# A fixed order of TensorE's work per head that begins three heads earlier in an attention block

## The chip, the cores and the metric

The kernel runs on one core of one Trainium2 chip. The metric is the device time of one execution in microseconds. A core has TensorE (PE, matrix products, with its weight loads shown as PEld), VectorE (DVE), ScalarE (ACT), GpSimd (POOL) and SyncE (SP). Here SP only issues DMA transfers; POOL issues some of them too and does a little elementwise work. The engines run side by side, each through its own list of instructions, and wait for each other by semaphores.

## The reference

The whole kernel is two transformer layers on `x` of 4 rows x 512 tokens x 512 channels: a gate, a state-space mixer, a gate, a mixture of experts, then a gate, attention, a gate and a feed-forward block. The change lies in the attention of the second layer:

```python
q = einsum('bsh,he->bse', x, w_q).reshape(b, sq, GROUPS, HPG, KVC)   # 4 groups x 4 heads x 128
kv = einsum('bsh,he->bse', x, w_kv)                                  # one key and one value per group
scores = einsum('bqgpd,bkgd->bgqpk', q, k) * SCALE
scores = where(causal, scores, -inf)
probs = softmax(scores, axis=-1)
ctx = einsum('bgqpk,bkgd->bqgpd', probs, v).reshape(b, sq, HEADS * KVC)
out = einsum('bse,eh->bsh', ctx, w_dense)                            # added to x
```

Here `x` stands for the gated input `h`. All numbers are 32-bit floats.

## The kernel before, in words

Attention runs over 64 heads in one Python loop, which is unrolled into the program: group `g` (0 to 3) outside, row of the batch `b` (0 to 3) within it, head of the group `i` (0 to 3) within that. This document counts them 0 to 63 in that order, so heads 12 to 15 are the last row of group 0, and head 16 is the first of group 1. A head is worked in these steps, which are spread over several turns of the loop:

- Queries. In group 0, `queries` makes the query of one head from `h` with four 128x512 products (L1726). From group 1 on, `two_queries` makes those of two heads with seven products of half size instead of eight (L1749), as a fast matrix product of 2x2 blocks; for it VectorE adds up the parts (L1752), and it needs sums of blocks of `h`, kept as `ht`, and of the weights, which POOL forms in `pair_weights` (L1518 to L1521) after the weights of the pair have been loaded (L1504). A call of `lead` records one half of a pair: four products, or three.
- Keys and values. `keys_` and `values` (L1699, L1710), once per group and row.
- Scores. `scores` makes four blocks of 128 queries (L1798, 128 to 512 columns, as the causal mask needs no more). VectorE adds the mask (L1801), takes the maximum (L1803), ScalarE the exponential (L128), VectorE scales (L1809, L1810) and transposes 32x32 blocks into `turned` (L1814). POOL then issues four transfers of `turned` to device memory (L1822).
- Between the blocks of scores, `nudge` adds a piece of the gates of later stages to VectorE and ScalarE (L259 to L333).
- Collecting. A later turn loads the transposed probabilities back as `pT` (L1840). This load is written to come after the last instruction recorded on POOL, and there are two `pT` buffers.
- Context. Three turns after the scores, `context` multiplies `pT` with the values (L1867), and ScalarE copies the result to `cx` (L1878). When the fourth head of a row is there, `dense` multiplies the four contexts with `w_dense` in four parts (L1886), each of which VectorE adds to `x` (L1894).

The order of the instructions on each engine is chosen when the program is built, by priority and by modelled readiness of operands, except where the code binds it. `after(nc.tensor)` binds an instruction behind the last one recorded on TensorE. `in_turn()` does so when the flag `even[0]` is set, and is wrapped around the paired queries, scores, contexts and dense parts. With the flag set, TensorE's order is the order in which the loop records the work, and three things differ from before: `ahead` records the queries of later heads in halves and the next row's keys and values, each in a fixed place after the scores of a head; one dense part is recorded per turn; and nothing is left to the builder. Without it, a row's dense product is recorded in one go, and queries go wherever the builder puts them. In this kernel the flag is set for groups 1 to 3, up to the last two heads.

The buffers that matter: `cx` has five buffers of its own, and four buffers `rr` that first hold results of the experts, loaded by `look_ahead` and added to `x` by `combine` during group 0; from group 1 on, contexts of rows 0 and 2 use the latter. `load_row` reloads `h` and `ht` of a row for the next group on SP's queue, at places given by a small table in the loop.

Of the kernel before, what the change touches and what calls it, by code (L numbers as in the profile page):

```python
# [19 lines left out]
B, T, C = 4, 512, 512  # L20
NC = C // P
# [24 lines left out]
HEADS, GROUPS, KVC = 16, 4, 128  # L46
# [37 lines left out]
def block_kernel(ctx: ExitStack, tc: tile.TileContext, a: dict, out: bass.AP):  # L84
    nc = tc.nc

    @contextmanager
    def after(*engines):

        with ExitStack() as es:  # L90
            for e in engines:
                last = next(
                    (i for i in reversed(nc.cur_bb.bb.instructions) if i.engine == e.engine), None
                )
                if last is not None:
                    es.enter_context(tc.issue_after(last))
            yield
# [48 lines left out]
    def ps_tp(name):  # L146
        return ps.tile([P, 512], F32, tag="tp", name=name, bufs=2)
# [755 lines left out]
    with ExitStack() as ph:  # L903
        right = dict(bufs=1, side="right", reuse_waits="tile")
        wx = early.enter_context(tc.tile_pool(name="ssm_wx", **right))
        even = early.enter_context(tc.tile_pool(name="ssm_even", **right))
# [211 lines left out]
        def start_tile(w, t):  # L1118
            u = Tile_()
            u.w, u.t = w, t  # L1120
            u.tok = slice(t * P, (t + 1) * P)
            u.first, u.last = t == 0, t == NT - 1

            u.zs = []
            for hh in range(2):
                pz = ps_mm("pz")
                for k in range(NC):
                    nc.tensor.matmul(  # L1128
                        pz,
                        lhsT=w.h[:, k, u.tok],  # L1130
                        rhs=wzt[:, k, hh * 512 : (hh + 1) * 512],
                        start=(k == 0),
                        stop=(k == NC - 1),
                    )
                zs = sm.tile([P, 512], F32, tag="zs", name="zs", bufs=3)
                act(zs, pz, AF.Silu)
                u.zs.append(zs)
            return u
# [209 lines left out]
        u = start_tile(w, 0)  # L1348
# [6 lines left out]
        for b in range(B):  # L1355
# [6 lines left out]
            for t in range(NT):  # L1362
# [97 lines left out]
                old, u = u, nxt  # L1460
# [100 lines left out]
    with tc.tile_pool(name="moe_w2", bufs=1, reuse_waits="tile") as wm:  # L1561
# [33 lines left out]
        n = len(nc.cur_bb.bb.instructions)  # L1595
# [15 lines left out]
    with att as ph:  # L1611
# [70 lines left out]
        even = [False]  # L1682

        def in_turn():
            return after(*[nc.tensor] * even[0])
# [34 lines left out]
        def new_q(i):  # L1720
            return sm.tile([P, T], F32, tag=f"q{i % 2}", name="qT", bufs=2)

        def queries(u, i):
            pq = ps_tp("pq")
            for k in range(NC):
                nc.tensor.matmul(  # L1726
                    pq,
                    lhsT=u.wq[:, i // 2, k, i % 2 * KVC : (i % 2 + 1) * KVC],
                    rhs=u.hk[:, k, :],
                    start=(k == 0),  # L1730
                    stop=(k == NC - 1),
                )
            qT = new_q(i)
            nc.scalar.mul(qT, pq, SCALE)
            return qT
# [95 lines left out]
        def new_pT():  # L1831
            return sm.tile([P, QUAD, SLOTS, SQ], F32, tag="pT", name="pT")
# [12 lines left out]
        def context(u, prs):  # L1845

            if isinstance(prs, list):
                pT = new_pT()
                for qi, pr in enumerate(prs):
                    n = (qi + 1) * P  # L1850
                    ptp = ps_tp("ptp")
                    for kj in range(qi + 1):
                        nc.tensor.transpose(
                            ptp[:, kj * P : (kj + 1) * P], pr[:, kj * P : (kj + 1) * P], ident
                        )
                    nc.any.tensor_copy(
                        pT[:, :, 3 * qi : 4 * qi + 1, :].rearrange("p r k j -> p k r j"),
                        ptp[:, :n].rearrange("p (k r j) -> p k r j", r=QUAD, j=SQ),
                    )
            else:  # L1860
                if id(prs) not in back:
                    collect()
                pT = back.pop(id(prs))
            pctx = ps_acc("pctx")
            with in_turn():
                for kj in range(NT):
                    nc.tensor.matmul(  # L1867
                        pctx[:, kj * P :].rearrange("p (q r j) -> p q r j", r=QUAD, j=SQ),
                        lhsT=u.v[:, kj, :],
                        rhs=pT[:, :, 4 * kj : 10 + kj : 3, :].rearrange("p r q j -> p q r j"),  # L1870
                        start=(kj == 0),
                        stop=(kj == NT - 1),
                    )
            if u.g == 0 or u.b % 2 or (u.g, u.b) == (GROUPS - 1, 2):
                cx = sm.tile([P, T], F32, tag="cx", name="cx", bufs=5)
            else:
                cx = cb.tile([P, T], F32, tag=f"rr{len(u.ctxT) % 2}", name="cx", bufs=2)
            nc.scalar.copy(cx, pctx)  # L1878
            u.ctxT.append(cx)
# [40 lines left out]
        heads_ = [(g, b, i) for g in range(GROUPS) for b in range(B) for i in range(HPG)]  # L1920

        def begin(n):
            g, b, i = heads_[n]
            if (g, b) not in groups:
                groups[g, b] = start_group(g, b, weights[g])
            u = groups[g, b]
            if i == 0 and not hasattr(u, "kT"):
                keys_(u)
                values(u)
            if g == 0:  # L1930
                return u, queries(u, i)
            if (g, b, i) == (1, 0, 0):
                lead(n)
                lead(n)
            return u, qs.pop((g, b, i))

        def lead(s):
            g, b, i = heads_[s]
            if (g, b) not in groups:
                groups[g, b] = start_group(g, b, weights[g])  # L1940
            if (g, b, i) not in making_q:
                making_q[g, b, i] = two_queries(groups[g, b], i // 2)
                qs[g, b, i] = next(making_q[g, b, i])
            else:
                qs[g, b, i + 1] = next(making_q.pop((g, b, i)))
# [28 lines left out]
        ready, held = begin(0), []  # L1974
        for n, (g, b, i) in enumerate(heads_):
            u, qT = ready
            if g == 0 and i == 0 and b + 1 < B:
                combine(b + 1, (0, 1))
                look_ahead(b + 1, (2, 3))
            if g == 0 and i == 3 and b + 2 < B:  # L1980
                look_ahead(b + 2, (0, 1))
            if g == 2 and i == 0 and b < 3:
                to, name = ((ffg_d, "gateT"), (ffu_d, "upT"), (ffd_d, "downT"))[b]
                nc.sync.dma_start(out=to, in_=a[name])
            s = n + ({2: 6} if g else {0: 4, 3: 5} if b == B - 1 else {}).get(i, len(heads_))
            if s < len(heads_):
                hs[heads_[s][:2]] = load_row(heads_[s][1])
            if loading:
                at, rest = loading.pop()
                pairs_w[at] = next(rest)  # L1990
            if (b, i) == (B - 1, 0) and g + 1 < GROUPS:
                weights[g + 1] = load_group(g + 1)
            pair = ((B - 1, 0), (B - 1, 3)) if g == 0 else ((B - 2, 3), (B - 1, 1))
            if (b, i) in pair and g + 1 < GROUPS:
                at = g + 1, pair.index((b, i))
                loading.append((at, pair_weights(*at)))
                next(loading[0][1])
            if n + 1 < len(heads_):
                ready = begin(n + 1)
            if g == 0 and i == 2 and b + 1 < B:  # L2000
                act.use(act.EXP)
                h = gated(2, b + 1, x[b + 1], gp, tag="h", name=f"h2_{b + 1}")
                hs[0, b + 1] = h, None
                act.use(act.LOG_EXP)
                mix(b + 1, h)
            even[0] = g > 0 and (g, b, i) < (GROUPS - 1, B - 1, 2)
            prs = scores(u, i, qT)
            if g == 0 and i == 1 and b + 1 < B:
                with after(nc.scalar):
                    combine(b + 1, (2, 3))  # L2010
            ahead(n)
            held.append((u, prs))
            if len(held) > 3:
                settle()
            dense_parts(2 if g == GROUPS - 1 and (b, i) >= (2, 2) else 1)
            if n == len(heads_) - 2:
                last_row_over = [
                    i for i in nc.cur_bb.bb.instructions if i.engine == nc.scalar.engine
                ][-1]
# [13 lines left out]
    with ExitStack() as ph:  # L2033
# [96 lines left out]
        with tc.If(n_odd > 0):  # L2130
            with ExitStack() as gen:
                wl = gen.enter_context(tc.tile_pool(name="ff_gen", bufs=2, **right))
                for b in range(B):
                    h = gated(3, b, x[b], gp, tag="h", name=f"h4_{b}")
                    hd = []
                    for i in range(NFF):
                        cs = slice(i * P, (i + 1) * P)
                        pv = []
                        for name in ("gateT", "upT"):
# [5 lines left out]
                            for k in range(NC):  # L2145
                                nc.tensor.matmul(
                                    pv[-1], lhsT=w[:, k, :], rhs=h[:, k, :],
                                    start=(k == 0), stop=(k == NC - 1),
# [7 lines left out]
                    for m in range(NC):  # L2156
# [6 lines left out]
                        for i in range(NFF):  # L2163
                            nc.tensor.matmul(
                                po, lhsT=w[:, i, :], rhs=hd[i], start=(i == 0), stop=(i == NFF - 1)
# [71 lines left out]
```

## Time and profile before

| what | value |
|---|---|
| time, median of 3 runs | 2247.05 us (2238.36, 2247.05, 2247.62) |
| the profiled execution: its time, its span | 2251.16 us, 2248.9 us |
| granted TensorE clock in the profiled execution, mean | 0.972 |
| attention's first and last score-side matmul on PE (queries of group 0; dense of group 3) | from 1135.6, to 2001.9 us |
| first paired query of group 1 | 1324.7 us |
| the costliest group of matmuls, dense L1886 | 227.9 us busy |

The profile was taken by the hardware profiler on one execution. Times are from the start of the span. A row of the timeline gives start, duration, engine, line, operation, output and inputs, shape and count, and in brackets how long the engine had been idle before it and what ended that. On TensorE each 32-bit matmul leaves two records, so four matmuls are "x8". The windows view gives for stretches of time the busy time of each engine with its number of instructions, then the granted TensorE clock, the mean busy share of the 16 DMA engines and the rate in GB/s.

### The profile page before, as it was taken

Reading aid. Unit: us, or ns where it says so; the run is one execution under the profiler, and the core shown is the slowest. Engines: PE = TensorE matmul, PEld = TensorE weight load, DVE = VectorE, ACT = ScalarE, POOL = GpSimd, SP = SyncE. Lnnn points to the kernel's source line nnn. Section 1 sums busy time; section 2 is a strip of 40 time slices with the busy share of each in tenths; the row PEclk is TensorE's granted clock in tenths of the full one; section 3 lists DMA queues with packets and bytes.
Section 4 is the critical chain, followed back from the end, with each engine's and each line's share of the span. In section 5 each row is a group of like instructions: output and inputs, shape, how many; then the busy total and the mean of one; then the engine's idle time right before and its main releaser. Section 6 shows DMA issues by size and latency. Waiting matters only on the chain.

```text
span 2248.9 us, 24719 instructions
## 1 busy us (share of the span) xinstructions
PE 2130.9 (95%) x7858; PEld 1292.5 (57%) x7858; DVE 1586.8 (71%) x3207; ACT 953.9 (42%) x1875; POOL 495.0 (22%) x668
## 2 busy tenths in 40 slices
PE   5879999999999999999988998999999999999998
PEld 2545565555665444444444555666666666568887
DVE  8698889989753557576579875788788866655332
ACT  4575666665842233333155432333333322333221
POOL 4022232322322111222133222212212221200000
PEclk9989989999999999999989998999999999999999
DMA  7542241342333457988578675777777665521100
GB/s 261 182 138 68 94 163 67 116 152 76 131 127 126 145 201 274 370 297 303 201 235 269 214 255 186 211 213 224 209 221 235 193 206 165 206 104 38 38 19 20
DMA packets 125512, 390.99 MB, mean 174 GB/s; under 512 B 15360, under 2 KB 36224, under 8 KB 111872
## 3 DMA queue, kind: packets, MB, share of 16 engines
q1 hardware_dynamic: 90560, 249.60, 32.1%
q0 software_dynamic: 32512, 135.55, 19.3%
q10 hardware_dynamic: 2304, 4.20, 0.5%
q8 instruction: 65, 1.06, 0.2%
q14 instruction: 71, 0.58, 0.1%
HBM read 363.07 MB, written 116.39 MB: 213 GB/s over the span
## 4 chain that ended last, share of the span: by engine, by line
PE 43%; DVE 4%; DMA 1%; ACT 1%; issue 1%; POOL 0%; SPq 0%; DVEq 0%; POOLq 0%
PE pd L1886 10%; PE pq L1749 6%; PE pctx L1867 6%; PE psc L1798 5%; PE pv L1710 2%; PE pk L1699 2%; PE pfo L2067 2%; PE pfo L2066 2%; PE pfg L2066 2%; PE pfg L2067 2%; PE pfu L2066 2%; PE pfu L2067 2%; PE pq L1726 1%; DMA pT<-turned 1%; DVE turned L1814 1%; DVE nmax L1803 1%
## 5 line engine op out<-in xcount | busy, mean ns | idle before, releaser
L128 ACT ACTIVATE pr<-psc,nmax 128x128 f32<-128x128 f32 (+3 forms) x256 | 134.3, 526 | 345.3 <-DVE nmax L1803 344.8
L1822 POOL DMA_DIRECT2D turned<-turned x248 | 135.7, 554 | 579.2 <-DVE turned L1814 491.3
L1886 PE MATMUL pd<-cx,wd 128*128 128x512 f32 x512 | 227.9, 593 | 0.0
L1798 PE MATMUL psc<-kT,qT 128*128 128x128 f32 (+3 forms) x512 | 158.6, 447 | 15.4 <-ACT pr L128 15.3
L1894 DVE TENSOR_TENSOR xr<-xr,pd 128x512 f32<-128x512 f32 x64 | 43.9, 686 | 176.3 <-PE pd L1886 176.2
L1057 PE MATMUL pc<-h,wxb 128*128 128x512 f32 x320 | 148.3, 619 | 5.8 <-DVE h L406 4.9
L1867 PE MATMUL pctx<-pT,v 128*128 128x512 f32 (+3 forms) x512 | 149.9, 436 | 2.9 <-DMA pT<-turned 2.9
L1886 PEld LDWEIGHTS pd<-cx,wd 128*128 128x128 f32 x512 | 93.9, 191 | 100.2 <-issue 98.6
L1867 PEld LDWEIGHTS pctx<-pT,v 128*128 128x128 f32 x512 | 96.5, 192 | 67.1 <-issue 40.8
L847 PE MATMUL po<-w,yT 128*128 128x512 f32 x296 | 134.1, 593 | 0.2 <-ACT yT L840 0.2
L814 PE MATMUL pg<-w,hT 128*128 128x512 f32 x296 | 134.0, 593 | 0.0
L825 PE MATMUL pn<-w,hT 128*128 128x512 f32 x296 | 133.3, 592 | 0.0
L1798 PEld LDWEIGHTS psc<-kT,qT 128*128 128x128 f32 x512 | 87.2, 194 | 68.8 <-issue 25.8
L1803 DVE TENSOR_REDUCE nmax<-psc 128x1 f32<-128x128 f32 (+3 forms) x256 | 119.8, 477 | 0.7
L1814 DVE STREAM_TRANSPOSE turned<-pr 128x128 f32<-128x128 f32 x248 | 119.3, 495 | 0.3
L1128 PE MATMUL pz<-wzt,h 128*128 128x512 f32 x256 | 115.9, 602 | 0.3 <-ACT st L1229 0.3
L1276 PE MATMUL po<-wot,yT 128*128 128x512 f32 x256 | 115.1, 603 | 0.0
L1057 PEld LDWEIGHTS pc<-h,wxb 128*128 128x128 f32 x320 | 61.5, 197 | 78.1 <-issue 72.3
L1810 DVE TENSOR_SCALAR pr<-pr,rsum 128x128 f32<-128x128 f32 (+3 forms) x256 | 103.9, 409 | 0.9
L1749 PE MATMUL pq<-ht,wq 128*128 128x256 f32 x384 | 100.3, 385 | 2.8 <-DVE us L1752 2.8
L1171 ACT ACTIVATE lm<-lm,cs 128x128 f32<-128x128 f32 x256 | 81.9, 390 | 22.1 <-DMA lm<-cs 19.5
L825 PEld LDWEIGHTS pn<-w,hT 128*128 128x128 f32 x296 | 54.8, 190 | 61.7 <-issue 61.7
(367 smaller groups left out, 4522.2 us busy)
## 6 DMA issues: line engine op xcount, KB each, us to landing
w<-in_w1x SPq DMA_DIRECT2D x76, 1024.0 KB
turned<-turned POOLq DMA_DIRECT2D x248, 208.0 KB, 4.0
pT<-turned POOLq DMA_DIRECT2D x62, 832.0 KB, 7.5
w<-in_w2x SPq DMA_DIRECT2D x38, 1024.0 KB
wb<-in_b1x SPq DMA_DIRECT2D x38, 512.0 KB
lm<-cs SPq DMA_DIRECT2D x32, 512.0 KB
kt<-in_fT SPq DMA_DIRECT2D x62, 256.0 KB
ek<-ek SPq DMA_DIRECT2D x62, 256.0 KB
```

The costliest lines, as they stand in the source:

```text
L128: nc.scalar.activation(*args, **kw)
L825: nc.tensor.matmul(pn, lhsT=hT[:, k, :], rhs=self.w1[s][1][:, k, :], start=(k == 0), stop=(k == NC - 1))
L1057: nc.tensor.matmul(pc, lhsT=wxb[:, k, m * P : (m + 1) * P], rhs=h[:, k, :], start=(k == 0), stop=(k == NC - 1),)
L1749: nc.tensor.matmul(out_, lhsT=w[:, c], rhs=xs[:, c], start=(c == 0), stop=(c == 1))
L1798: nc.tensor.matmul(psc[:, :n], lhsT=qT[:, qi * P : n], rhs=u.kT[:, :n], start=True, stop=True)
L1803: nc.vector.tensor_reduce(nmax, psc[:, :n], AX.X, ALU.max, negate=True)
L1814: nc.vector.transpose(blocks[:, :, 3 * qi : 4 * qi + 1, :].rearrange("p c k j -> p k c j"), pr)
L1822: nc.gpsimd.dma_start(out=d[:, :, r].rearrange("c i s -> i c s"), in_=blocks[r * SQ : (r + 1) * SQ].rearrange("i c k j -> i c (k j)"),)
L1867: nc.tensor.matmul(pctx[:, kj * P :].rearrange("p (q r j) -> p q r j", r=QUAD, j=SQ), lhsT=u.v[:, kj, :], rhs=pT[:, :, 4 * kj : 10 + kj : ...
L1886: nc.tensor.matmul(po, lhsT=dense_w[u.g, m][:, i], rhs=u.ctxT[i], start=(i == 0), stop=(i == HPG - 1),)
L2066: nc.tensor.matmul(out_, lhsT=w, rhs=xs[0], start=first_, stop=False)
L2067: nc.tensor.matmul(out_, lhsT=w, rhs=xs[1], start=False, stop=last_)
```

## The change

`even[0]` is now set at the top of a turn instead of before the scores, and from head (0, 3, 1) on, that is from the second head of group 0's last row. The simple queries of group 0 are wrapped in `in_turn()` too. Since `ahead` now records the first pair of group 1 in the turns of heads 13 and 14, the two calls of `lead` at the first head of group 1 are gone, and what that pair needs is recorded one head earlier: the reload of row 0, and the load and the sums of the first pair's weights (the second pair's from head 15 to head 14). Row 2 of group 0 now has its dense parts spread over four turns, so its contexts live longer; they go to the `rr` buffers.

```diff
         def queries(u, i):
             pq = ps_tp("pq")
-            for k in range(NC):
-                nc.tensor.matmul(
+            with in_turn():
+                for k in range(NC):
+                    nc.tensor.matmul(
...
-            if u.g == 0 or u.b % 2 or (u.g, u.b) == (GROUPS - 1, 2):
+            if u.b % 2 or (u.g, u.b) < (0, B - 2) or (u.g, u.b) == (GROUPS - 1, 2):
                 cx = sm.tile([P, T], F32, tag="cx", name="cx", bufs=5)
             else:
                 cx = cb.tile([P, T], F32, tag=f"rr{len(u.ctxT) % 2}", name="cx", bufs=2)
...
             if g == 0:
                 return u, queries(u, i)
-            if (g, b, i) == (1, 0, 0):
-                lead(n)
-                lead(n)
             return u, qs.pop((g, b, i))
...
             u, qT = ready
+            even[0] = (0, B - 1, 1) <= (g, b, i) < (GROUPS - 1, B - 1, 2)
...
-            s = n + ({2: 6} if g else {0: 4, 3: 5} if b == B - 1 else {}).get(i, len(heads_))
+            s = n + ({2: 6} if g else {B - 2: {3: 5}, B - 1: {3: 5}}.get(b, {})).get(i, len(heads_))
...
-            pair = ((B - 1, 0), (B - 1, 3)) if g == 0 else ((B - 2, 3), (B - 1, 1))
+            pair = ((B - 2, 3), (B - 1, 2)) if g == 0 else ((B - 2, 3), (B - 1, 1))
...
-            even[0] = g > 0 and (g, b, i) < (GROUPS - 1, B - 1, 2)
             prs = scores(u, i, qT)
```

More of the change, by code (lines that the diff above doesn't have):

```diff
@@ L1724, in queries @@
             pq = ps_tp("pq")
-            for k in range(NC):
-                nc.tensor.matmul(
[L1727 to L1732, printed above, removed]
+            with in_turn():
+                for k in range(NC):
+                    nc.tensor.matmul(
+                        pq,
+                        lhsT=u.wq[:, i // 2, k, i % 2 * KVC : (i % 2 + 1) * KVC],
+                        rhs=u.hk[:, k, :],
+                        start=(k == 0),
+                        stop=(k == NC - 1),
+                    )
             qT = new_q(i)
```

## The prediction

> **What bounds the kernel now.** I read the page's busy shares first, then the same numbers by stage, then, for the stage of the change, what TensorE waits for, and last the rows of TensorE, POOL and VectorE there.
>
> ```profile
> span 2248.9 us, 24719 instructions
> PE 2130.9 (95%) x7858; PEld 1292.5 (57%) x7858; DVE 1586.8 (71%) x3207; ACT 953.9 (42%) x1875; POOL 495.0 (22%) x668
> ```
>
> TensorE (PE) is the busiest engine, but 95% is a mean over stages. The windows view (busy time of each engine, granted clock, DMA share and rate) shows where it is less:
>
> ```profile
> 1312.72:1404.50 91.78, 79.41 (x277) 50.38 (x276) 68.06 (x171) 29.85 (x75) 24.71 (x43) 0.93 0.62 210
> 1440.00:1531.80 91.80, 91.80 (x357) 60.26 (x356) 71.17 (x198) 35.59 (x88) 23.41 (x42) 1.00 0.72 216
> 1345.53:1348.94 3.41, 0.69 (x4) 0.26 (x2) 3.02 (x11) 1.66 (x4) 0.00 (x0) 1.00 0.96 344
> 1348.94:1352.36 3.42, 3.32 (x8) 2.67 (x9) 2.00 (x5) 0.00 (x0) 2.18 (x4) 0.50 0.95 317
> 1389.90:1393.31 3.41, 1.87 (x5) 1.52 (x6) 1.81 (x5) 0.00 (x0) 1.86 (x4) 0.50 1.02 428
> 1393.31:1396.73 3.42, 3.42 (x10) 2.70 (x9) 0.42 (x1) 0.38 (x1) 0.33 (x1) 0.50 1.01 405
> ```
>
> The first row is the stretch that the change rewrites: from the end of head 12's scores to the first key product of group 1's second row (heads counted 0 to 63 over group, row, head). PE idles in it and runs at a granted clock of 0.93. The second row, as long, lies in group 1, where the fixed order already holds: PE never stops. So a microsecond saved in the first stretch should reach the end. What PE waits for between 1312 and 1410 us:
>
> ```profile
> PE pq L1749 <- DVE qT L1752: 7.3, 1, 7.3
> PE pq L1749 <- DVE us L1752: 2.8, 1, 2.8
> PE psc L1798 <- ACT pr L128: 1.2, 2, 0.8
> PE pk L1699 <- ACT pr L128: 1.0, 1, 1.0
> ```
>
> Both large waits stand at group 1's paired query products: VectorE's sums for them are queued behind softmax and gate work, while the 32 matmuls of row 2's dense product, 1355.51 to 1369.25, pass in one block in which VectorE has little to do. To two digits the five waits are 7.35, 2.83, 0.81, 0.44 and 0.95: 12.38 us. The timeline rows of PE and of POOL that I use:
>
> ```profile
> 1310.56 2.32 PE L1798 MATMUL psc<-kT,qT 128*128 128x128 f32 x8
> 1349.04 2.07 PE L1749 MATMUL pq<-ht,wq 128*128 128x256 f32 x4 [2.83 <-DVE us L1752]
> 1355.51 13.90 PE L1886 MATMUL pd<-cx,wd 128*128 128x512 f32 x32
> 1391.44 2.08 PE L1749 MATMUL pq<-h,wq 128*128 128x256 f32 x4 [7.35 <-DVE qT L1752]
> 1312.95 2.18 POOL L1822 DMA_DIRECT2D turned<-turned  x4 [17.68 <-DVE turned L1814]
> 1317.91 0.56 POOL L1840 DMA_DIRECT2D pT<-turned  x1 [2.78 <-PE pctx L1867]
> 1340.69 0.55 POOL L1822 DMA_DIRECT2D turned<-turned  x1 [10.68 <-DVE turned L1814]
> 1341.25 0.74 POOL L1521 TENSOR_TENSOR wq<-wq 128x256 f32<-128x256 f32 x1
> 1341.91 0.57 POOL L1840 DMA_DIRECT2D pT<-turned  x1
> ```
>
> POOL issues in order, and a `pT` load there (the transposed probabilities that a context needs) can stand behind a `turned` store that waits for VectorE's transposes of a later head.
>
> **What the stage loses.** Work in it, from row distances (a group's start to the next group's): two queries of group 0 at 3.44, six heads of scores at 2.16, seven contexts at 2.16, three pairs of queries at 6.03, keys 3.44, values 3.57, dense 13.74: 6.88+12.96+15.12+18.09+3.44+3.57+13.74 = 73.8 us. It took 91.78, so 18.0 are lost: 12.38 idle, and half of the 3.32+1.87+3.42 us that PE worked in the three windows at clock 0.50, 4.3; the other 1.3 go with the five restarts. That is the most this stage can give back.
>
> **The order.** The new order on PE has the same matmuls up to the same key product: contexts 8 and 9, query 14, scores 13, first half of pair 16, context 10, query 15, scores 14, second half of pair 16, keys, context 11, a dense part, scores 15, half of pair 18, values, context 12, a part, and so on. Pair 16 gets two heads of lead, and the dense block becomes four parts of 3.44. So the waits of 7.35 and 2.83, and the 2.2 on exponentials, go: VectorE's 68.06 us lie beside 73.8 of matmuls instead of being bunched. PE gets 11.2, 17.2, 14.8, 10.3 and 11.2 us per head for heads 13 to 17, VectorE needs some 11 for each (scores 1399.75 to last transpose 1411.09: 11.3).
>
> **What is late next.** The first pair's weight sums (L1518 to L1521) stand one head earlier on POOL, now behind head 11's `turned` stores and ahead of head 12's first; and the `pT` load of head 10, which went out at 1317.91, now stands behind that first store and L1521. The store waits for VectorE. There the last reciprocal of head 12 starts at 1321.26, the scaling follows (0.19+0.40), then the four transposes (1.68, from the row at 1323.74, which the new order has ahead of head 13's mask): 1323.55. POOL starts 0.29 later (as 1325.42 to 1325.71), and its step from store to load is 1.22 (1340.69 to 1341.91): load out at 1325.06. The load in that same position, at 1341.91, landed after 5.7 us, the one at 1380.76 after 5.4; so at 1330.8. PE comes to context 10 at 1312.72+2.16+2.16+3.44+2.16+3.45 = 1326.1. A new wait of 4.7 us, with query 15, scores 14 and all later heads queued behind it. Bounds: the shortest `pT` landing in the trace is 4.5, the slowest near here 10.5 (at 1382.96, beside two 1 MB loads): 3.5 to 9.5. I take 5.7, the row in the same position; row 1's loads, which met the stores at 1325.71, now go out only after query 15.
>
> By the Trainium skill, "DMA: Bandwidth & Descriptors", section "Anatomy of one DMA — SWDGE (gpsimd) path", a transfer takes 2.0 us plus bytes over 436 GB/s, so an estimate of 3.95 us for 832 KB and a wait of 2.9. The trace disagrees: none landed under 4.5.
>
> **The clock after it.** A 3.41 us window with PE busy for 0.69 was followed by one at 0.50, and one at 0.50 with 1.87 busy by another. On that grid (1325.05, 1328.46, 1331.87) the new wait leaves 1.0 busy in the first window and 1.1 in the second, so PE works at half clock from 1330.8 to 1335.3 and loses 2.2; with another phase 1.2 to 2.9. With 0.3 for the restart the new loss is 7.2 (5 to 12.5).
>
> In the Trainium skill, "TensorE: Matmul & The Clock Gate", section "Why this matters for your kernels", gaps over about 3 us bring the half clock, for one window: 1.7 us here. The trace agrees that a gap costs clock, but 2.83 us was already enough.
>
> **The other edits.** Row 2's context copies go to the buffers of the expert results (last read by the transposes at 1271.01): the same ACT copy, 0. Row 0's reload and the first pair's load are written one head earlier, but SP's queue keeps them in place: 0. The second pair's 0.5 MB load still follows query 15, which now ends near 1336.4; landing in 9.3 (its 1325.17 load) at 1346, then POOL's sums after head 14's stores end near 1350.8; pair 18 needs them at 1353.3: hidden by 2.5 us. If that cover goes, PE waits by the excess. SP holds `ht` of row 1 behind it, needed at 1376. The contexts after 10 are covered: head 13's load, again behind a store and L1521, is out near 1361 and wanted at 1370.
>
> **Sum.** 18.0 − 7.2 = 10.8 us. The profiled execution took 2251.16 (span 2248.9), 4.1 over the median 2247.05: 2240.4 as profiled, 2236.2 against the median; I say 2236.
>
> **Rivals.**
> - No new wait: the transposes of head 12 or its transfers come 5 us sooner. Then all 18.0 return: 2229. Against it: VectorE has no idle row from 1308 to 1346, so head 12 can't be sooner. 8%.
> - A slow transfer: `pT` takes 8 to 10.5. Loss 9.5 to 12.5, gain 5.5 to 8.5: 2238.5 to 2241.5. For it, 10.5 stands in the trace; against, it had 1 MB loads beside it. 12%.
> - VectorE becomes the bound: 68 us of it in 81 us is 84% against 78% in group 1, and with several waits in line a queue head holds the rest. The idle of PE moves rather than goes: gain 0 to 7, around 2243. Also where the order does nothing. 5%.
> - Slower: the hold on POOL repeats. If VectorE takes longer per head than PE does, the store of head n+2 holds each context as it holds context 10: at contexts 10 to 13 four times 7.2, 28.8 against the 18.0: 2258. It decides once VectorE needs more than 11.2 us a head several heads long. Group 1's 100% under this order speaks against it. 5%.
>
> **How the numbers follow.** The forecast has 70%, its own range 2233 to 2239. The bound of 0.5%, about what a measurement here can tell from no change, is 11.2 us, at 2235.8, so it cuts the forecast: 42 points beyond, as a landing 0.4 us sooner or a shorter stretch at half clock is enough for that, and 28 short. With the first rival 50% faster; with the slow transfer and the moved idle 45% the same; 5% slower. The range 2230 to 2243 holds the forecast, the slow transfer, part of the moved idle, and a run's scatter (2238.36 to 2247.62).
>
> **What would show it.** Right: no wait at L1749 on L1752 in this stretch; pd in groups of 8 rows; one PE gap of 4 to 6 us before `pctx`, ended by the DMA of `pT`, 13.4 us after head 12's scores; half clock for one or two windows there; the stretch at 81 us. Wrong: the gap missing or above 9 us, gaps before later contexts, a gap at pair 18 on L1520, or time moved outside the stretch.

## The result, and the profile after

The changed kernel took a median of 2231.03 us in 12 runs (2226.19 to 2236.79). The kernel before took 2242.70 in its 12 runs beside it (2237.88 to 2254.39); the three runs known ahead, with a median of 2247.05, are among those. The medians are 11.7 us apart. The ratio, which is that of the means, is 0.9943, 95% interval [0.9926, 0.996]: 12.8 us less, between 9.0 and 16.6. A second series, with 27 runs of the kernel before, gave 0.9951 [0.9933, 0.9969], 11.0 us less. So the change saves time beyond doubt; on which side of 0.5% the saving lies, neither series tells.

The profiled execution took 2229.05 us. Its page:

```profile
span 2227.1 us, 24718 instructions
PE 2115.8 (95%) x7858; PEld 1283.1 (58%) x7858; DVE 1584.9 (71%) x3207; ACT 952.4 (43%) x1875; POOL 500.2 (22%) x668
```

The same number of matmuls, and 15.1 us less of PE's busy time, of which only 3.1 are in the stretch that the change rewrites; a second execution of the kernel before, at 2120.8 busy, shows that much of the rest is scatter. The windows view of that stretch, from the end of head 12's scores to the first key product of group 1's second row (called the stage from here on), of PE's idle time in it, and of the context behind that:

```profile
1300.24:1382.08 81.84, 76.35 (x277) 48.75 (x276) 66.25 (x168) 29.65 (x75) 26.58 (x43) 0.96 0.68 221
1314.35:1317.76 3.41, 0.00 (x0) 0.00 (x0) 3.41 (x11) 1.83 (x5) 2.21 (x4) 0.87 0.78 192
1319.52:1323.81 4.29, 4.29 (x9) 2.45 (x10) 3.67 (x8) 0.78 (x2) 0.32 (x1) 0.52 0.77 316
```

The stage takes 81.84 us; it took 91.78. PE's busy time in it fell from 79.41 to 76.35 and its granted clock rose from 0.93 to 0.96. What is left of idle time is almost all in one piece, from 1314.35 to 1319.52. The second row shows its first 3.41 us, in which VectorE does not stop; the context behind it then runs at a clock of 0.52. PE's waits in the stage are two in all:

```profile
PE pctx L1868 <- DMA pT<-turned: 5.2, 1, 5.2
PE psc L1799 <- ACT pr L128: 0.3, 1, 0.3
```

Both waits at the paired queries (7.35 and 2.83) are gone. (Every line from L1727 on has moved down by one.) A new wait of 5.17 us stands before a context. The timeline of PE, then of POOL, then of VectorE:

```profile
1313.32 1.03 PE L1750 MATMUL pq<-ht,wq 128*128 128x256 f32 x4
1319.52 4.45 PE L1868 MATMUL pctx<-pT,v 128*128 128x512 f32 x8 [5.17 <-DMA pT<-turned]
1323.81 3.60 PE L1727 MATMUL pq<-h,wq 128*128 128x512 f32 x8
1337.58 3.60 PE L1887 MATMUL pd<-cx,wd 128*128 128x512 f32 x8
```

```profile
1302.66 1.56 POOL L1518 TENSOR_TENSOR wq<-wq 128x256 f32<-128x256 f32 x1
1304.20 1.69 POOL L1519 TENSOR_TENSOR wq<-wq 128x256 f32<-128x256 f32 x1
1305.86 0.76 POOL L1520 TENSOR_TENSOR wq<-wq 128x256 f32<-128x256 f32 x1
1312.53 0.55 POOL L1823 DMA_DIRECT2D turned<-turned  x1 [5.91 <-DVE psc L1802]
1313.09 0.74 POOL L1521 TENSOR_TENSOR wq<-wq 128x256 f32<-128x256 f32 x1
1313.76 0.57 POOL L1841 DMA_DIRECT2D pT<-turned  x1
```

```profile
1302.02 1.69 DVE L259 TENSOR_TENSOR_SCAN num<-decay,ekv 128x512 f32<-128x512 f32 x1
1303.63 1.68 DVE L322 SCALAR_TENSOR_TENSOR den<-den,rec 128x1024 f32<-128x1024 f32 x1
1310.54 1.68 DVE L1815 STREAM_TRANSPOSE turned<-pr 128x128 f32<-128x128 f32 x4
```

POOL's rows are the hold: it stands idle for 5.91 us at head 12's first `turned` store, and head 10's `pT` load is in line behind the store and L1521. (The view names L1802 as what ended the idle time, the VectorE row right behind the four transposes; those end at 1312.22, as VectorE's rows show.) The load goes out at 1313.76, and PE begins at 1319.52. That the load itself was ready some 11 us earlier is shown by the first experiment below. VectorE's rows show why the store waited longer than it might have: beside POOL's L1518 and L1519 the scan L259 and L322 took 1.69 and 1.68 us, and the two sums twice their usual 0.73.

Single executions scatter more than the effect, so the experiments below are also compared by two lengths from their profiled executions: the stage (here from the end of the last score row, so 91.62 before and 81.68 after), and the rest, from the stage's end to the end of the span. The scatter comes largely from ahead of the stage: attention's first key product began between 1115.1 and 1127.0 us, and from there to the stage's start it took 184.6 to 190.9, in kernels with and without the change. The stage repeats to 0.3 us: 91.62 and 91.89 for the kernel before, 81.68 and 81.54 for the changed one. The rest was 844.4 and 841.9 before, 845.0 and 844.9 after, so it repeats to some 3.

Where a stage below is compared with "the kernel before" or "the changed kernel", it is with the mean of these two profiles, 91.76 and 81.61, unless a figure is given.

| kernel | ratio to before, 95% | stage us | stage and rest us |
|---|---|---|---|
| before, again | 1.0006 [0.9986, 1.0026] | 91.89 | 933.8 |
| changed, again | 0.9951 [0.9933, 0.9969] | 81.54 | 926.4 |
| `pT` collected first | 0.9964 [0.9946, 0.9982] | 83.35 | 928.1 |
| queries in another PSUM buffer | 0.9945 [0.9927, 0.9963] | 81.36 | 924.9 |
| both | 0.9935 [0.9916, 0.9953] | 77.84 | 919.0 |
| both, row 2's dense product in one block | 0.9925 [0.9904, 0.9946] | 77.10 | 920.6 |
| both, nothing bound before group 1 | 0.9957 [0.9939, 0.9975] | 81.30 | 922.5 |
| changed, dense product in one block | 1.0005 [0.9988, 1.0022] | 83.19 | 936.2 |
| changed, nothing bound before group 1 | 1.0004 [0.9984, 1.0024] | 82.70 | 931.3 |
| changed, simple queries not bound | 0.996 [0.9943, 0.9977] | 81.69 | 926.9 |
| before, dense parts spread | 1.0007 [0.999, 1.0024] | 88.13 | 932.3 |
| before, `pT` collected first | 0.9987 [0.9966, 1.0008] | 90.95 | 932.1 |

### The profile page after: what moved, and what is told of

Read it like the earlier page. It is cut to its first block, busy times and chain, and to the rows that moved or that the text cites. A ratio compares the mean times of both kernels' runs of the same rounds, so it can differ in the third digit from the quotient of the medians.

```text
span 2227.1 us, 24718 instructions
## 1 busy us (share of the span) xinstructions
PE 2115.8 (95%) x7858; PEld 1283.1 (58%) x7858; DVE 1584.9 (71%) x3207; ACT 952.4 (43%) x1875; POOL 500.2 (22%) x668
```

## The experiments

The theory: the gain is the two waits at the paired queries, and what is left is `pT` in line on POOL. The rivals are named with each run. First the same two kernels again.

> The kernel before once more, for a second profile of the stage between head 12's scores and the first key product of group 1's second row (91.78 us in the first). If the saving lies in that stage alone, it is 91 to 93 us here too, with the waits of about 2.8 and 7.4 us at L1749 again, whatever the span; if earlier stages or the profile's luck made the difference, it will lie elsewhere or change by several us.

> The changed kernel once more. My theory (the saving is this stage: waits at the first paired queries gone, one new wait before context 10): stage 81 to 83 us, one gap of 4.5 to 6 us before pctx, ratio 0.994 to 0.997. The rival that something outside the stage changed too: the part of the span ahead of head 12's scores, or behind the first key product of row 1, differs from before by more than 2 us in the same direction in both pairs of profiles, and the ratio is under 0.994.

Measured: five waits of 0.44, 0.81, 0.94, 2.83 and 7.36 before, two of 0.32 and 4.89 after. The waits belong to the kernels, not to an execution. The rival's signs came out mixed. The part ahead of the stage was shorter in the changed kernel in both pairs of profiles, by 12.5 us (1312.88 to 1300.40) and 4.2 (1308.55 to 1304.34); the ratio, at 0.9951, was not under 0.994. What the first is worth is taken up under what stays open.

**Is the place of `pT` on POOL the cause of the new wait?** One line puts the load ahead of the pair's sums:

```diff
             if loading:
                 at, rest = loading.pop()
+                collect(1)
                 pairs_w[at] = next(rest)
```

> The changed kernel with one call added: head 10's (and later each) pT load is recorded ahead of the weight sums, so on POOL it no longer stands behind the store of head 12. Theory of the place on POOL: the gap of 5.2 us before context 10 disappears; but query 15 needs one of two tp PSUM buffers, which VectorE's sums of pair 16 free at 1322.5 in the changed kernel's profile, 8 us after PE would be there, less what VectorE gains; so I expect a wait of 3 to 5 us at L1727 on a VectorE sum instead, and a gain of only 1 to 3 us over the changed kernel. Rival, the wait is the whole cost: 5.2 and some 2 of half clock, 7 us gained. Rival, the transfer itself is the cost and not its place: the gap stays at 5 us, no gain.

The load went out right behind head 11's stores, and the sums after it:

```profile
1319.12 0.56 POOL L1841 DMA_DIRECT2D pT<-turned  x1 [0.20 <-issue]
1319.69 0.74 POOL L1518 TENSOR_TENSOR wq<-wq 128x256 f32<-128x256 f32 x1
```

PE's waits in the stage were then:

```profile
PE pq L1727 <- DVE us L1753: 4.9, 1, 4.9
PE psc L1799 <- ACT pr L128: 1.4, 1, 1.4
```

The load went out 2.6 us after the stage's first context instead of 13.5, and the wait before the context is gone, so the place on POOL was its cause. But the next matmul, the query of head 15, waited as long: it needs a PSUM buffer whose last reader is VectorE's sum of pair 16 (L1753), and those sums stand behind head 13's softmax. The stage did not get shorter (83.35 us), where a gain of 1 to 3 us was expected.

**And that buffer alone?** With `pT` where the change has it:

```diff
         def queries(u, i):
-            pq = ps_tp("pq")
+            pq = (ps_mm if even[0] else ps_tp)("pq")
```

> The changed kernel, with the simple queries of heads 14 and 15 in a PSUM buffer of the ps_mm kind, and pT loaded where the change has it. Theory (two waits stand one behind the other, and pT's place on POOL comes first): the wait of about 5 us before head 10's context stays at 4.5 to 5.5, the stage (end of head 12's scores to the first key product of group 1's second row) stays at 81 to 82 us, and the ratio at 0.994 to 0.997. Rival (the PSUM buffer alone is the cost, since lifting both gave 77.8): the stage falls to 77 to 79.

```profile
PE pctx L1868 <- DMA pT<-turned: 4.2, 1, 4.2
PE psc L1799 <- ACT pr L128: 1.0, 1, 1.0
```

The stage took 81.36, the ratio 0.9945 [0.9927, 0.9963]: like the changed kernel. The wait is still the load's, a little under what the theory allowed. Taking away either wait alone gives nothing, as the other is behind it or ahead of it.

**Both edits together.**

> As the run with the pT load first, and the queries of heads 14 and 15 also use the four mm PSUM buffers instead of the two tp ones. If the two waits stand one behind the other, as I think, both are gone here and PE has no gap over 1 us in the stage: 74 to 76 us, 6 to 8 us better than the changed kernel, ratio to before about 0.990 to 0.992. If the pT load was the whole cost, the same as the run before it; if VectorE is the bound of the stage, no better than 1 to 3 us and waits at scores on exponentials.

```profile
PE psc L1799 <- ACT pr L128: 1.8, 1, 1.8
```

That is the only wait left in the stage. The stage took 77.84, 3.8 less than in the changed kernel. That is about half of the 6 to 8 expected, and the wait is one on an exponential, over the 1 us that was allowed. The rest took 841.2. In the changed kernel the load's place makes another `pT` wait in group 2's last row (2.89 us at 1725.45, on POOL behind a store and L1521 again); here that one is gone too.

**Is it the spread dense parts that bring the gain?** First in the kernel before the change, only the two edits that spread row 2's product (the contexts go to the `rr` buffers as in the change):

```diff
-                if not even[0]:
+                if not even[0] and (old.g, old.b) != (0, B - 2):
                     dense_parts(NC)
```

> The kernel before, with one part of the change: row 2's dense product recorded in four parts over four turns (with the change's context buffers), nothing bound before group 1 and no early pair. If spreading the dense parts was what saved time, the stage falls to 82 to 85 us. My theory asks for the query pair to be early as well: VectorE's sums of pairs 16 and 18 are still made at the last moment, so waits of about 3 and 6 to 7 us at L1749 stay, the stage is 88 to 92 us, and the time is within 3 us of before.

```profile
PE pq L1749 <- DVE qT L1752: 6.3, 1, 6.3
PE pq L1749 <- DVE us L1752: 2.8, 1, 2.8
```

The parts passed as groups of 8 rows between other work, and the wait of 7.35 fell by 1.0, to 6.35. The stage took 88.13, 3.6 less; the ratio, 1.0007 [0.999, 1.0024], shows no gain of that size. Most of the 3.6 is clock: PE's work between the wait of 2.83 and the next context took 2.69 us here and 4.32 in the first profile of before, that between the longer wait and the next context 5.29 instead of 6.15. Then the other way round, the changed kernel with row 2's product in one block:

```diff
-                if not even[0]:
+                if not even[0] or (old.g, old.b) == (0, B - 2):
                     dense_parts(NC)
```

> The changed kernel, with row 2's dense product in one block again, all else bound and early. If the early pair and the fixed order of queries are what saved time, the stage stays at 81 to 83 us and the time within 2 us of the changed kernel. If the block also hurts, as I think, because VectorE runs dry during its 13.7 us and has more to catch up after it, new waits follow it: 4 to 8 us of the 10 are lost, in the stage or within a row after it.

The whole gain was gone, more than the 4 to 8 us expected: 1.0005 [0.9988, 1.0022]. But the stage took 83.19, only 1.6 more than the changed kernel; most of the loss lies behind it. There the trace has a wait that the changed kernel does not, in POOL's rows and PE's, both in group 1's last row:

```profile
1524.76 0.55 POOL L1823 DMA_DIRECT2D turned<-turned  x1 [14.22 <-DVE turned L1815]
1525.32 0.74 POOL L1521 TENSOR_TENSOR wq<-wq 128x256 f32<-128x256 f32 x1
1525.99 0.57 POOL L1841 DMA_DIRECT2D pT<-turned  x1
```

```profile
1532.87 3.74 PE L1868 MATMUL pctx<-pT,v 128*128 128x512 f32 x8 [4.12 <-DMA pT<-turned]
```

In the changed kernel (its second profile) the same step on POOL is not behind a store:

```profile
1507.84 0.73 POOL L1521 TENSOR_TENSOR wq<-wq 128x256 f32<-128x256 f32 x1
1508.51 0.57 POOL L1841 DMA_DIRECT2D pT<-turned  x1
```

The builder had put L1521 one store later, and the load, recorded behind it, went along. So this run does not tell what the block costs. The version with both edits cannot be caught in that way, and with it the block was tried again:

> The version with pT collected first and the queries in ps_mm (77.84 us in the stage, 919.0 from the stage's start to the end), but with row 2's dense product in one block as before the change. Theory (the block alone cost the changed kernel 1.6 us in the stage, and the rest of its loss was another hold of pT on POOL): the stage takes 78.5 to 80.5, no wait over 2 us stands at a later context, and from the stage's start to the end it takes 919 to 923. Rival (the block leaves VectorE without work and then late, as the prediction read the kernel before): a wait of 3 to 7 us at the paired queries returns, and the stage takes 81 to 85.

```profile
PE psc L1799 <- ACT pr L128: 1.8, 1, 1.8
PE pk L1699 <- ACT pr L128: 0.6, 1, 0.6
```

```profile
1338.59 13.90 PE L1887 MATMUL pd<-cx,wd 128*128 128x512 f32 x32
```

```profile
1306.82:1383.91 77.09, 74.69 (x276) 47.37 (x275) 65.21 (x163) 28.92 (x72) 22.90 (x40) 1.00 0.70 227
```

The block is there, 13.90 us in one piece. The wait of 1.8 stands ahead of it, and behind it comes only one of 0.6, on an exponential, before the key product that ends the stage. The stage took 77.10, 0.7 less than with the parts spread, at a granted clock of 1.00. That is less than either expectation had. From the stage's start to the end it took 920.6, as the theory said. Spreading row 2's product is not what the gain comes from.

**Is it the binding, or the earlier recording?** In the changed kernel, work is recorded in the new places, but nothing is bound behind TensorE's last instruction until group 1 (`bound` is set where `g > 0`):

```diff
-            return after(*[nc.tensor] * even[0])
+            return after(*[nc.tensor] * (even[0] and bound[0]))
...
-                with after(nc.tensor):
+                with after(*[nc.tensor] * bound[0]):
```

> The changed kernel, recording all the same work in the same early turns, but binding nothing on TensorE before group 1. If recording pair 16, keys and values early is what saved time, the stage is 81 to 84 us. If the binding is, waits come back wherever the builder's order meets an operand not ready, 8 us or more in all, and most of the 10 us are lost: time within 4 us of before.

No gain, 1.0004 [0.9984, 1.0024]. But the stage took 82.70, with no wait at a paired query, and again a `pT` load stood behind a store and L1521 in group 1's last row (a wait of 3.34 us at 1531.72). So here too the loss is partly that of POOL, and the same edit was made in the version with both others:

> The same version, with the work recorded in the same places but nothing bound behind TensorE's last instruction before group 1: the builder may place it. Theory (the place of recording, with the dense parts and the pair's halves spread, brings the gain, and the binding hardly any): the stage takes 77.5 to 80, and from its start to the end 919 to 923. Rival (the builder draws the pair's halves or dense parts together, and their sums on VectorE are late again): waits of 2 to 7 us at the paired queries, the stage at 82 to 87.

```profile
PE pq L1750 <- DVE us L1753: 2.5, 1, 2.5
PE psc L1799 <- ACT pr L128: 0.8, 1, 0.8
PE pk L1699 <- ACT pr L128: 0.7, 1, 0.7
```

The stage took 81.30, between the two expectations, with a wait at a paired query as the rival had it: the builder put the last two products of pair 18's first half (1361.01) and the second half (1365.36) back to back, and the second had to wait for VectorE's sums of the first. From the stage's start to its end at the span's it took 922.5, 3.5 more than the bound version, which is the stage's 3.5. So of the 13.8 us between the kernel before (91.62) and the bound version (77.84), 10.3 need no binding: they come with the new places of recording and the two edits above. In this version, binding is worth the other 3.5.

**Do the simple queries need to be bound?** The changed kernel without `in_turn()` in `queries`:

> The changed kernel, with the simple queries of group 0 not bound. If their place matters, PE meets query 15 while its PSUM buffer is still held by VectorE's sums, or scores waiting for exponentials: one wait of 4 to 7 us at L1727 in place of that before context 10, stage 82 to 85 us, 1 to 4 us slower than the changed kernel. If it doesn't, stage 81 to 82.

```profile
PE pq L1726 <- DVE us L1752: 3.4, 1, 3.4
PE psc L1798 <- ACT pr L128: 2.2, 2, 1.6
```

The wait changed its place, not the time: the builder put the query of head 15 first, where it waited 3.42 for L1752, and `pT` landed meanwhile. The stage took 81.69, the same as with it.

**Was the hold on POOL in the kernel before too?** The kernel before, with the line of the first experiment alone:

> The kernel before the change, with pT collected ahead of the first pair's weight sums, and nothing else. Theory (its waits of 7.35 and 2.83 us hang on VectorE's sums for the paired queries, not on POOL): the 7.35 stays at 6.5 to 8, the stage takes 88.5 to 92, the ratio is 0.997 to 1.001. Rival (the hold of pT on POOL was in the kernel before too, and is what its waits come from): the 7.35 falls under 4, the stage to 83 to 86, the ratio to 0.994 to 0.997.

```profile
PE pq L1749 <- DVE qT L1752: 8.6, 1, 8.6
PE pk L1699 <- ACT pr L128: 2.4, 1, 2.4
```

Not as the cause of these waits: the one for the paired sums stayed and grew by 1.2 (to 8.57, over the 8 that the theory allowed), the one of 2.83 went, another grew. The stage took 90.95, the ratio is 0.9987 [0.9966, 1.0008]. In this stage only the changed kernel pays for the hold. Further on the kernel before pays for one too: in group 2's last row its `pT` load went out at 1739.50, behind a store and L1521, and PE waited 2.40 us for it at 1747.38 (1.78 in the second profile). With this line that wait is gone.

## Why the prediction was right or wrong

**What the stage loses, and what goes.** Right. The waits of 7.35 and 2.83 went, of the 2.2 on exponentials 0.32 is left, the dense product shows in four separate parts, each a row of "x8", and the stage takes 81.84 us where 81 was said: 9.9 less, where the sum said 10.8.

**What is late next.** Right in its place and cause, and close in size. Measured from the stage's start at 1300.24, the load goes out 13.52 us after it (12.34 was worked out), PE can begin 5.76 later (5.7), and PE comes to the context after 14.11 (13.4): a wait of 5.17 for 4.7. The mis-sized term is the load's departure, by 1.2 us. VectorE's four transposes began at 1310.54, 10.30 after the stage's start; the prediction had them end at 10.83, so begin 9.15 after it. Of those 1.15 us, 0.96 is what the scan L259 and L322 took beyond the 1.21 and 1.20 that they take in the kernel before, with no sum on POOL beside them:

```profile
1314.51 1.21 DVE L259 TENSOR_TENSOR_SCAN num<-decay,ekv 128x512 f32<-128x512 f32 x1
1315.64 1.20 DVE L322 SCALAR_TENSOR_TENSOR den<-den,rec 128x1024 f32<-128x1024 f32 x1
```

POOL's L1518 and L1519 beside them took 1.56 and 1.69 instead of 0.73 and 0.72. The prediction moved the sums on POOL as if they cost VectorE nothing.

**The clock after it.** Right: 2.2 was predicted. Eight rows of context 10 took 4.29 us instead of 2.16, so 2.1 went, and PE was back at full clock from 1323.81. By the Trainium skill, "TensorE: Matmul & The Clock Gate", section "Why this matters for your kernels", the estimate was one window at half clock, 1.7 us by its length here; with a gap of 5.17 us this trace cannot speak on the page's 3 us.

**The transfer.** The load landed after 5.76 us, as the row in the same position had it. The estimate of 3.95 us from "DMA: Bandwidth & Descriptors" in the Trainium skill, section "Anatomy of one DMA — SWDGE (gpsimd) path", was 1.8 short.

**The other edits.** Right: no wait at pair 18 on POOL's sums, none at later contexts of the stage, none for `ht`.

**The cause of the 7.35 wait.** Wrong in part. The prediction read it from the dense block, "in which VectorE has little to do". With the block back and the other waits lifted, no such wait returned, and with the block spread in the kernel before, 6.35 of 7.35 stayed. By elimination it is the earlier place of the pairs' halves, with other heads' work between them, that removes it, though no run moved the pairs alone. Once they stand there, and the two later waits are lifted, the spread is worth under a microsecond (77.84 with it, 77.10 without).

**The sum against the median.** This step failed. "2240.4 as profiled, 2236.2 against the median" took the profiled execution as 4.1 over the median of three runs. Over 12 runs the median is 2242.70, so that execution stood 8.5 over it: the base of the sum was 4.35 us too high. With the same 10.8 the right base gives 2251.16 − 8.5 − 10.8 = 2231.9, and 2231.03 was measured. That these two lie so close is partly luck. The stage gave 9.9, 0.9 less than the sum said, and the medians are 11.7 apart, so nearly 2 us of the saving are not the stage's, and the sum put all that lies outside the stage at nothing.

**The numbers.** The bound of 0.5% was the other mistake: it was taken as what a measurement here can tell from no change, but the interval is 0.17% to each side, and a saving of 0.57% is easily told from no change. The forecast of 10.8 us is 0.48% of 2247.05, just short of that bound. By putting 28 of the forecast's 70 points on the near side of it, and 2236 as well, the prediction called it close to no change where its own mechanism meant a plain gain. The forecast's own range, 2233 to 2239, does not hold the time; the whole range, 2230 to 2243, holds it by 1 us. None of the rivals happened: in the stage the hold on POOL makes PE wait once.

**What stays open.** The two profiles of each kernel show 10.1 us less in the stage on the mean, and 8.3 less from the stage's start to the end, while the two ratios mean 12.8 and 11.0. So 2.7 to 4.5 us may lie ahead of the stage. There, executions of one kernel differ by several microseconds: in the four profiles of kernels built on the one before, the stage starts at 1307.6 to 1312.9 us, in the ten built on the changed one at 1300.4 to 1316.7. The means, 1310.2 and 1306.0, lie the right way, but the scatter is as large, and no run here separates a part of the change from it.

## What to carry to other kernels

A wait that a new order removes uncovers the next in line, and two that stand one behind the other pay only when both go: here neither edit alone gave anything, and both gave 3.8 us of the stage. In a queue that issues in order, as POOL's rows show its own to do, ask of every load what stands ahead of it, as a store that waits for another engine holds loads whose data are ready, and a small edit elsewhere can bring that about much later: the block recorded again at 1342.66 made a load late at 1532.87. And compare the stage that an edit touches before comparing spans: stages repeated to 0.3 us where whole executions differed by 10. Then look behind the stage as well, as that block's loss stood there. The version with both edits and the block (2225.84 us, 0.9925 [0.9904, 0.9946]) had the lowest median of all; its interval overlaps with that of the changed kernel, its stage, at 77.10 against 81.54 and 81.68, does not.

## What the runs showed of the hardware that was not expected

- POOL and VectorE hold each other up. L322 took 1.20 us with no addition on POOL, 1.68 beside one addition on POOL, and 3.45 where three of them ran one behind the other (both edits together; the additions took 0.74, 0.72 and 0.71 there):

```profile
1305.66 3.45 DVE L322 SCALAR_TENSOR_TENSOR den<-den,rec 128x1024 f32<-128x1024 f32 x1
```

  The 2.25 us more are about the time from the first addition's start to the last one's end, 2.1. The Trainium skill, "GPSIMD Engine Reference", section "1. Specifications", says that GpSimd shares its SBUF interfaces with VectorE and contends with VectorE's instructions of two SBUF inputs; L322 has two, and the trace agrees. Which of the two lost was not always the same: here it was VectorE alone in one kernel, and both in the other.
- Idle time of PE of 4.85 us before the query of head 15 (`pT` collected first) had the four matmuls behind it take 6.63 us instead of 3.60: 3.0 more, where a gap of 5.17 cost 2.1 in the changed kernel. A gap of 2.83 ahead of three paired products was followed by 4.32 us for them in the kernel before, and by 2.69 where only its dense parts were spread (the second row below). The length of a gap alone does not set what it costs in clock.

```profile
1338.70 6.63 PE L1727 MATMUL pq<-h,wq 128*128 128x512 f32 x8 [4.85 <-DVE us L1753]
1343.72 1.13 PE L1749 MATMUL pq<-ht,wq 128*128 128x256 f32 x4 [2.83 <-DVE us L1752]
```
